# The last bias of a mixer layer: added by a TensorE pass, or into x by accumulating DMAs

## The chip, the cores and the metric

The kernel runs on one core of a Trainium2 chip. The metric is device time in microseconds (us) of one execution. Engines are named as in the profile: PE is TensorE's matmul side and PEld its weight loads, DVE is VectorE, ACT ScalarE, POOL GpSimd, and SP SyncE, which here only issues DMAs. An engine works through its instructions in the order in which they were written for it and waits on semaphores for what others produce. DMAs issued by SP and by POOL are carried out by the same 16 DMA engines. Only POOL issues the DMAs that add to their destination instead of overwriting it.

## The reference, cut to what matters

The input is 8 images of 128 x 128 pixels and 64 channels, in float32. The first layer is an attention along rows and columns. The second, the mixer, has two halves for each image, and the change lies in the very last term:

```python
h  = _pw(_ln(x, g1, b1), w_te, b_te)                  # 64 -> 128 channels
F  = fft2(h);  fc = gelu(_pw([re F, im F], w_fc, b_fc))
x1 = x + _pw(real(ifft2(fc)), w_tp, b_tp)
h2 = _pw(_ln(x1, g2, b2), w_fe, b_fe)                 # 64 -> 128 channels
d  = gelu(conv3x3_depthwise(h2, w_dw) + b_dw)
return x1 + _pw(d, w_fp, b_fp)                        # 128 -> 64, and the bias b_fp
```

`_pw` is a matrix product over the channels plus a bias. `b_fp` has 64 values; each is added to one channel of every pixel.

## The kernel before, in words

**Attention** (to about 1277 us) goes over tasks of 32 rows or columns. In its first four tasks it also runs the four steps of `preparation`, which fold weights and biases into a packed table in DRAM. The step `first` (from line 176) splits `b_fp` into three bf16 parts, so that their sum keeps the precision, repeats them for 8 rows and stores them in DRAM as `thirds` (line 192).

**The mixer** (from line 679) works image by image, in two parts that overlap: while `transforms(b)` runs for image b, mostly on PE, `mlp(b-1)` runs for the image before, mostly on DVE. One image's x, 128 x 128 x 64 in float32, stays in SBUF (32 KB on each of 128 partitions; a partition is a column of the image), in two buffers that take turns.

`transforms`: `along_w` and `along_h` (PE) are the Fourier transforms, `channels` (PE, L859), `bend` (ACT, L869) and `hermite` (POOL, L875) the middle layer with its gelu, `project`, `inverse_h` and `inverse_w` (PE) the way back, and `add` (DVE, L935) adds the result to x. This makes x1.

`mlp` takes x1 in 16 chunks of 8 lines, and a small 17th for the last line:

- `norm` sums each pixel's channels on DVE (L949, L950) and takes the inverse roots.
- `scale` (POOL, L1060) multiplies 8 lines of x by the roots, `turn` (PE) transposes them, `keep_x` (ACT) copies them, `expand` (PE) and `keep_e` (ACT) make h2.
- The depthwise convolution has nine taps. ACT does the first; one or two more are made by ACT as products, which DMAs add up (`gather`, POOL, L1153: an accumulating DMA of 512 KB from SBUF to SBUF); the other six or seven are `tap` on DVE (L1159).
- `bend` (ACT, L1206) is the gelu, and `shrink` (PE, L1215 ff.) the last product. It begins with a bf16 matmul over three rows (L1219), which writes the bias to all of the chunk's output in PSUM; 32 float32 matmuls (L1225) then accumulate onto it.
- `add` (DVE, L1230) reads PSUM and x, writes `ot`, and `store` (SP) sends it out. The output of chunk k is lines 8k-1 to 8k+6, one line behind its input.

In the last image half of the chunks do their convolution on PE instead.

The order on each engine is written by a planner. Every step is a task with an estimated cost, the tasks it follows, a due time, and the buffer slots that it takes and frees (`SLOTS`: four PSUM slots "mm" are shared by seven kinds of step, `shrink` among them). The planner repeatedly looks for the earliest start on each engine and, of those that could start within 0.3 us of it, takes the one due first. Due times come from the constants in line 47: image b's work begins at b times `PERIOD`, group i of the transforms is due `GROUP0 + GROUP * i` later, inverse group i `BACK0 + BACK * i`, chunk k of the mlp `CHUNK0 + CHUNK * k`. `lag` is the time that a DMA is taken to need until it lands. The planner's costs decide only the order; on the chip the engines wait for semaphores.

Of the kernel before, what the change touches and what calls it, by code (L numbers as in the profile page):

```python
# [22 lines left out]
F32 = mybir.dt.float32  # L23
BF16 = mybir.dt.bfloat16
I32 = mybir.dt.int32
AF = mybir.ActivationFunctionType
ALU = mybir.AluOpType
# [4 lines left out]
P = 128  # L32
C = 64
# [10 lines left out]
BY_DMA, BY_DMA_LAST = (1, 2), 1  # L44


PERIOD, GROUP0, GROUP, BACK0, BACK, CHUNK0, CHUNK, STAY, LOADX = 262.0, 0.5, 10.2, 174.8, 4.7, 22.4, 13.9, 0.0, -10.2
CH = 8
LN = 16

# [79 lines left out]
    return out  # L130


def preparation(nc, pool, ps, ident, prm, marks, packed, thirds):

    (g1, b1, g2, b2, w_te, b_te, w_fc, b_fc, w_tp, b_tp, w_fe, b_fe, w_dw, b_dw, w_fp, b_fp) = prm
    HW = float(P * P)
    v, dma = nc.vector, nc.sync.dma_start
# [5 lines left out]
    def cut(rows, cols):  # L143
        at[0] += cols
        return tmp[0:rows, at[0] - cols : at[0]]
# [18 lines left out]
    dma(out=f["wdw"], in_=w_dw.rearrange("a b o d -> d (a b o)"))  # L164
    dma(out=f["bdw"], in_=b_dw.unsqueeze(1))
    dma(out=f["wfp"], in_=w_fp)
    bfp = cut(3, C)
    dma(out=bfp, in_=b_fp.unsqueeze(0).to_broadcast([3, C]))

    split = pool.tile([3, CH * C + P + 3 * C], BF16, tag="split", name="split", bufs=1)  # L170
    dma(out=wrow, in_=w_dw.rearrange("a b o d -> (o a b) d").unsqueeze(0).to_broadcast([P, 9, HID]))
    dma(out=f["mark"], in_=marks[0:2, 0:8])
    dma(out=f["line"], in_=marks[:, 8 : 8 + P])
    hold = {}

    def first():
        parts = split[:, CH * C + P :].rearrange("p (n c) -> p n c", n=3)
        row = cut(3, C)
        for n in range(3):
            v.tensor_copy(parts[:, n, :], bfp)  # L180
            if n < 2:
                v.tensor_tensor(bfp, bfp, parts[:, n, :], ALU.subtract)
        v.tensor_scalar_mul(row, parts[:, 0, :], ident[0:3, 0:1])
        for n in range(1, 3):
            v.scalar_tensor_tensor(
                out=row, in0=parts[:, n, :], scalar=ident[0:3, n : n + 1], in1=row, op0=ALU.mult, op1=ALU.add
            )
        v.tensor_copy(
            split[:, 0 : CH * C].rearrange("p (n c) -> p n c", n=CH), row.unsqueeze(1).to_broadcast([3, CH, C])
        )  # L190
        nc.gpsimd.memset(split[:, CH * C : CH * C + P], 1.0)
        nc.gpsimd.dma_start(out=thirds, in_=split[:, 0 : CH * C + P])

        v.tensor_copy(f["ident"], ident)
        v.tensor_scalar(cen, ident[0:C, 0:C], -1.0 / C, None, ALU.add)
        v.tensor_scalar_mul(f["wtpn"], f["wtp"], -0.5)
        v.tensor_scalar_mul(f["wtp"], f["wtp"], 0.5)

        p = hold["a"] = ps.tile([P, 8, P], F32, tag="ps", name="pa")
        nc.tensor.matmul(p[:, 0, 0:1], lhsT=wte, rhs=col[:, 1:2], start=True, stop=True)  # L200
        nc.tensor.matmul(p[:, 0, 1:2], lhsT=wfr, rhs=col[:, 3:4], start=True, stop=True)
        v.tensor_scalar(u, p[:, 0, 0:1], bte, HW, ALU.add, ALU.mult)
        v.tensor_scalar(f["bfe"], p[:, 0, 1:2], bfe0, None, ALU.add)
        v.tensor_scalar_mul(wfr, wfr, col[:, 2:3])
        v.tensor_scalar_mul(wte, wte, col[:, 0:1])
# [52 lines left out]
    return [first, second, third, fourth]  # L258


def attention(tc, nc, x, w_q, b_q, w_k, b_k, w_v, b_v, gamma, x2, xn, prm, marks, packed, thirds):
    NB = x.shape[0]
    with ExitStack() as ctx:
        const = ctx.enter_context(tc.tile_pool(name="a_const", bufs=1))
# [4 lines left out]
        late = ctx.enter_context(tc.tile_pool(name="a_late", bufs=2))  # L269
        xw = ctx.enter_context(tc.tile_pool(name="a_xw", bufs=6))  # L270

        ps = ctx.enter_context(tc.tile_pool(name="a_ps", bufs=4, space=PSUM))
# [18 lines left out]
        ident = const.tile([P, P], F32, tag="ident", name="ident")  # L291
# [47 lines left out]
        for n in range(3):  # L339
            v = const.tile([P, R, C + 1], F32, tag="v%d" % n, name="v")  # L340
# [270 lines left out]


        fetch(1)
        prepare = preparation(nc, late, ps, ident, prm, marks, packed, thirds)
        N = len(tasks)
        E = mybir.EngineType
        with tc.manual_schedule(engines={E.PE, E.Activation, E.DVE, E.Pool}):
# [58 lines left out]
                flush(1)  # L676


def mixer(tc, nc, x2, xn, tbl, packed, thirds, out):
    NB = out.shape[0]  # L680
    with ExitStack() as ctx:
        const = ctx.enter_context(tc.tile_pool(name="m_const", bufs=1))
# [8 lines left out]
        rw, cos, sin, nsin, cosn, sinn, nsinn, idw = (tb[:, P * i : P * i + P] for i in range(8))  # L691
        pk = const.tile([P, PACKED], F32, tag="pk", name="pk")
        nc.sync.dma_start(out=pk, in_=packed[:, 0:PACKED])
        bias = const.tile([3, CH * C + P], BF16, tag="bias", name="bias")
        nc.sync.dma_start(out=bias, in_=thirds)
        c = fields(pk, PARTS)
        ident, wplus, wminus, dc, bfc, wtp, wtpn, btp, e0, wfe = (
            c[n] for n in ("ident", "wplus", "wminus", "dc", "bfc", "wtp", "wtpn", "btp", "e0", "wfe")
# [98 lines left out]
        plan = Plan()  # L797
# [249 lines left out]
        class Mlp:  # L1047
# [30 lines left out]
            def blank(self):  # L1078
# [2 lines left out]
                    nc.gpsimd.memset(t[:, :, P + 1 : P + 2], 0.0)  # L1081
                nc.gpsimd.memset(self.ring[0][:, 0, 1 : P + 1], 0.0)

            def turn(self, k):
                xc = self.xc.pop(k)
                tp = self.ps["t", k] = ps_m.tile([P, 4, P], F32, tag="mm", name="tpn")
                for j in range(4):
                    nc.tensor.transpose(
                        tp[:, j, :], xc[:, 2 * j : 2 * j + 2, :].rearrange("p s c -> p (s c)"), ident
                    )  # L1090
# [124 lines left out]
            def shrink(self, k):  # L1215
                i0, i1, r0 = self.rows(k)
                acc = self.acc.pop(k)
                op = self.ps["o", k] = ps_m.tile([P, CH, C], F32, tag="mm", name="op")
                nc.tensor.matmul(  # L1219
                    op[:, i0:i1, :].rearrange("p i c -> p (i c)"), lhsT=bias[:, CH * C : CH * C + P],  # L1220
                    rhs=bias[:, i0 * C : i1 * C], start=True, stop=False,
                )
                for i in range(i0, i1):
                    for z in (slice(0, 64), slice(64, 128)):
                        nc.tensor.matmul(op[z, i, :], lhsT=acc[:, i, z], rhs=wfp, start=False, stop=i == i1 - 1)  # L1225

            def add(self, k):
                i0, i1, r0 = self.rows(k)
# [11 lines left out]
        def mlp(b):  # L1240
# [5 lines left out]
            start = plan.add("SP", 0.0, lambda: m.__init__(b), im.added, t0 - 5)  # L1246
            root = norm(lambda: m.x, lambda: m.st, lambda h: t0 - 4 + h / 4, lambda h: [start])
            m.done = []
            e, ext, keep_x, users = None, None, [], []
            ready = start if b else plan.add("POOL", 0.8, lambda: m.borders(), [start], t0 - 30)  # L1250
            if last:

# [2 lines left out]
            for k in range(P // CH + 1):  # L1255
# [4 lines left out]
                if k < P // CH:  # L1260
                    xc, xt, s = Slot("xc"), Slot("xt"), Slot("mm")
                    takes = (s,) if last else (s, xt)
                    a = plan.add("POOL", 1.5, lambda k=k: m.scale(k), [root[k // 8]], t - 14, takes=(xc,))
                    p = plan.add("PE", 0.5, lambda k=k: m.turn(k), [a], t - 10, "F", takes, (xc,))
                    wait = []
                    if last:
                        wait = [keep_x[-1]] if k else [ext]
                        for n in (2, 3):
                            wait = wait + (users[-n] if len(users) >= n else [])
                    x_ = plan.add("ACT", 0.95 if last else 0.6, lambda k=k: m.keep_x(k), [p] + wait, t - 9, frees=(s,))  # L1270
                    keep_x.append(x_)
# [11 lines left out]
                else:  # L1283
# [24 lines left out]
                    for n in range(1, 1 + by_dma):  # L1308
                        s = Slot("pr")
                        a = plan.add("ACT", 1.22, lambda k=k, n=n: m.product(k, n), [e, first], t - 1 + n, takes=(s,))  # L1310
                        read = [a]
                        if made is None:
                            made, slot = a, s
                        else:
                            made = plan.add(
                                "POOL", 1.0, lambda k=k, n=n: m.gather(k, n, 1), [a, made], t + 6 * n - 5, frees=(s,), lag=7.1
                            )
                    for n in range(1 + by_dma, 9):
                        g = plan.add(
# [3 lines left out]
                    last_e[(17 * b + k) % 3] = [g] + read  # L1323
                    if made is not None:
                        g = plan.add(
                            "POOL", 1.0, lambda k=k: m.gather(k, 1), [g, made], t + late + 4, frees=(slot,), lag=7.1
                        )
                    g = plan.add("ACT", 0.4 if small else 1.06, lambda k=k: m.bend(k), [g], t + late + 13 - 1.6 * by_dma)
                    t += late
                s, ot = Slot("mm"), Slot("ot")  # L1330
                p = plan.add("PE", 1.25, lambda k=k: m.shrink(k), [g], t + 15, "C", (s,), (acc,))
                d = plan.add("DVE", 0.7, lambda k=k: m.add(k), [p], t + 16, takes=(ot,), frees=(s,))
                m.done.append(d)
                plan.add("SP", 1.0, lambda k=k: m.store(k), [d], t + 16, frees=(ot,), lag=5.0)

# [8 lines left out]
@with_exitstack  # L1344
def attention_mixer_kernel(ctx: ExitStack, tc: tile.TileContext, x, w_q, b_q, w_k, b_k, w_v, b_v, gamma, *rest):
    nc = tc.nc
    *prm, tbl, marks, out = rest
    NB = x.shape[0]
    dram = ctx.enter_context(tc.tile_pool(name="dram", bufs=1, space=DRAM))
    x2 = [dram.tile([P, P, C], F32, tag="x2_%d" % b, name="x2_%d" % b) for b in range(NB)]  # L1350
    xn = [dram.tile([P, 2, C, 64], F32, tag="xn_%d" % b, name="xn_%d" % b) for b in range(NB)]
    packed = dram.tile([P, PACKED + ADDED], F32, tag="packed", name="packed")
    thirds = dram.tile([3, CH * C + P], BF16, tag="thirds", name="thirds")
    attention(tc, nc, x, w_q, b_q, w_k, b_k, w_v, b_v, gamma, x2, xn, prm, marks, packed, thirds)
    mixer(tc, nc, x2, xn, tbl, packed, thirds, out)


_INS = [
# [29 lines left out]
```

## Time and profile before

| | |
|---|---|
| three runs | 3218.33 us median, 3213.28 to 3226.0 |
| the profiled execution | 3221.41 us, of which 3219.6 is the span from the first to the last instruction |
| mean granted TensorE clock | 0.971 |
| busy: PE, DVE, ACT, POOL | 2944.8, 2548.9, 2100.1, 1561.0 us |
| attention, up to the first Fourier pass | 0 to 1277 us |
| one image of the mixer, in between | 229 to 237 us |
| from the last transform add to the end | about 140 us |

How to read what follows: a busy time is the time in which an engine worked; the rest it waited. A group's line gives the instruction's source line, engine, operation, output and inputs, shapes and count, then busy time, the mean of one in ns, the idle time just before, and who ended it. A waits line reads "engine tile line <- releaser: us in total, times, longest". The chain of waits is followed back from the last instruction of the program, at each step to what released it; it tells which work the end hung on. In a windows line the columns are the window, its length, the busy us (and number) of PE, PEld, DVE, ACT and POOL, the granted clock, the share of the DMA engines and GB/s.

### The profile page before, as it was taken

Reading aid. Unit: us, or ns where it says so; the run is one execution under the profiler, and the core shown is the slowest. Engines: PE = TensorE matmul, PEld = TensorE weight load, DVE = VectorE, ACT = ScalarE, POOL = GpSimd, SP = SyncE. Lnnn points to the kernel's source line nnn. Section 1 sums busy time; section 2 is a strip of 40 time slices with the busy share of each in tenths; the row PEclk is TensorE's granted clock in tenths of the full one; section 3 lists DMA queues with packets and bytes.
Section 4 is the critical chain, followed back from the end, with each engine's and each line's share of the span. In section 5 each row is a group of like instructions: output and inputs, shape, how many; then the busy total and the mean of one; then the engine's idle time right before and its main releaser. Section 6 shows DMA issues by size and latency. Waiting matters only on the chain.

```text
span 3219.6 us, 110523 instructions
## 1 busy us (share of the span) xinstructions
PE 2944.8 (91%) x50612; PEld 2142.9 (67%) x50612; DVE 2548.9 (79%) x2322; ACT 2100.1 (65%) x2744; POOL 1561.0 (48%) x1944
## 2 busy tenths in 40 slices
PE   7998888988888987999999899999899999999978
PEld 6877777777777776666576576575566575665644
DVE  4574747474756567719999999999999999999996
ACT  3665656565655655538868768768668678677654
POOL 1095959595958585414515415515415425335321
PEclk8999999999999998999999999999999999999989
DMA  6024242434333323232552653643634634634433
GB/s 174 23 95 129 99 120 95 128 97 136 108 107 120 95 94 135 101 123 40 144 134 50 157 110 66 158 93 73 161 83 89 156 84 93 151 77 81 96 62 75
DMA packets 222458, 339.17 MB, mean 105 GB/s; under 512 B 142879, under 2 KB 176296, under 8 KB 207528
## 3 DMA queue, kind: packets, MB, share of 16 engines
q0 software_dynamic: 32496, 154.84, 20.4%
q1 hardware_dynamic: 188728, 177.19, 19.4%
q8 instruction: 397, 6.50, 0.8%
q14 instruction: 69, 0.57, 0.1%
q10 hardware_dynamic: 768, 0.07, 0.0%
HBM read 137.40 MB, written 102.25 MB: 74 GB/s over the span
## 4 chain that ended last, share of the span: by engine, by line
PE 52%; DVE 33%; issue 6%; POOL 6%; ACT 1%; DMA 1%; SPq 0%; POOLq 0%; DVEq 0%; ACTq 0%
DVE acc L1159 23%; PE yp L422 6%; PE fcps L859 5%; PE e L452 4%; PE dps L927 3%; PE yps L914 3%; PE vps L400 3%; DVE m L457 3%; PE tp L367 3%; PE pq L381 3%; PE yps L916 3%; PE tpy L603 2%; POOL xb L563 2%; PE op L1225 2%; PE aps L819 2%
## 5 line engine op out<-in xcount | busy, mean ns | idle before, releaser
L1159 DVE SCALAR_TENSOR_TENSOR acc<-h,pk,acc 128x1024 f32<-128x1024 f32 x840 | 1332.6, 1591 | 34.8 <-ACT acc L1145 13.3
L875 POOL TENSOR_TENSOR gs<-gl 128x512 f32<-128x512 f32 (+2 forms) x272 | 418.7, 1593 | 245.3 <-ACT gl L869 234.4
L859 PE MATMUL fcps<-f,pk 128*128 128x512 f32 (+2 forms) x1088 | 499.4, 591 | 0.0
L457 DVE TENSOR_REDUCE m<-e 128x8 f32<-128x1024 f32 x256 | 300.9, 1211 | 207.0 <-PE e L452 206.4
L1153 POOL DMA_DIRECT2D acc<-pr x120 | 105.6, 880 | 644.8 <-DVE acc L1159 428.1
L869 ACT ACTIVATE gl<-fcps,pk 128x1024 f32<-128x1024 f32 (+2 forms) x272 | 291.1, 1074 | 118.1 <-PE fcps L859 95.6
L463 ACT ACTIVATE att<-e 128x1024 f32<-128x1024 f32 x256 | 259.7, 1024 | 165.3 <-PE e L452 161.5
L422 PEld LDWEIGHTS yp<-v,att 128*64 128x64 f32 x8192 | 270.3, 143 | 89.1 <-issue 42.2
L1060 POOL TENSOR_TENSOR xc<-x,st 128x512 f32<-128x512 f32 x128 | 183.7, 1440 | 286.5 <-DVE st L101 186.1
L859 PEld LDWEIGHTS fcps<-f,pk 128*128 128x128 f32 x1088 | 190.5, 190 | 197.3 <-issue 162.8
L452 PE MATMUL e<-kt,qt 32*128 32x128 f32 x4096 | 298.4, 288 | 23.8 <-DVE v L403 12.7
L422 PE MATMUL yp<-v,att 128*64 128x65 f32 x8192 | 298.3, 230 | 20.6 <-issue 18.7
L452 PE MATMUL e<-qt,kt 32*128 32x128 f32 x4096 | 297.0, 286 | 15.6 <-issue 13.5
L452 PEld LDWEIGHTS e<-kt,qt 32*128 32x128 f32 x4096 | 257.9, 191 | 44.4 <-issue 21.2
L452 PEld LDWEIGHTS e<-qt,kt 32*128 32x128 f32 x4096 | 255.3, 191 | 20.2 <-issue 13.9
L1149 ACT ACTIVATE pr<-h,pk 128x1024 f32<-128x1024 f32 x176 | 214.1, 1236 | 0.0
L899 PEld LDWEIGHTS gps<-pk,gs 128*64 128x64 f32 x4032 | 135.5, 141 | 116.5 <-issue 65.5
L403 DVE TENSOR_TENSOR v<-vps,bv 128x1024 f32<-128x1024 f32 x128 | 155.9, 1218 | 66.9 <-PE vps L400 66.8
L914 PE MATMUL yps<-tb,gt 128*64 128x128 f32 x1024 | 200.8, 278 | 3.0 <-DVE ot L1230 2.4
L400 PE MATMUL vps<-wv,xt 64*64 64x64 f32 x8192 | 158.9, 228 | 46.6 <-DVE m L457 27.7
L915 PE MATMUL yps<-tb,gt 128*64 128x128 f32 x1024 | 200.8, 278 | 0.0
L842 PE MATMUL fps<-tb,at 128*64 128x128 f32 x1008 | 196.3, 277 | 0.0
(226 smaller groups left out, 7424.5 us busy)
## 6 DMA issues: line engine op xcount, KB each, us to landing
acc<-pr POOLq DMA_DIRECT2D x120, 512.0 KB, 5.4
xb<-in_x_dram SPq DMA_DIRECT2D x32, 1024.0 KB
xn<-xn SPq DMA_DIRECT2D x32, 1024.0 KB
x<-x SPq DMA_DIRECT2D x32, 1024.0 KB
x<-xb POOLq DMA_DIRECT2D x30, 1024.0 KB, 6.0
out_dram<-ot SPq DMA_DIRECT2D x120, 256.0 KB
xn<-yw POOLq DMA_DIRECT2D x14, 2048.0 KB, 9.4
pr<-pr POOLq DMA_DIRECT2D x56, 512.0 KB, 6.4
```

The lines of the kernel that those rows point to most:

```text
L400: nc.tensor.matmul(vps[z, s, j, :], lhsT=self.xts[t][rows, j, z], rhs=wv[rows, :], start=True, stop=True)
L422: nc.tensor.matmul(yq[z, q, j, :], lhsT=att[:, q, j, z], rhs=self.v[:, r, :], start=True, stop=True)
L452: nc.tensor.matmul(e[:, q, j, :], lhsT=left[rows, 4 * a + j, :], rhs=right[rows, 4 * a + j, :], start=not msk, stop=j == 3 or not msk,)
L457: nc.vector.tensor_reduce(new.mneg[:, 2 * k : 2 * k + 2, 4 * a : 4 * a + 4], e1, AX.X, ALU.max, negate=True,)
L463: nc.scalar.activation(att, e2, AF.Exp)
L859: nc.tensor.matmul(ps[:, sgn, 0:n], lhsT=w[:, cols], rhs=fv, start=True, stop=not mean)
L869: nc.scalar.activation(gl[:, :, 0:n], ps[:, :, 0:n], AF.Gelu, bias=bfc[:, half : half + 1])
L875: nc.gpsimd.tensor_tensor(gs[:, 0:n], gl[:, 0, 0:n], gl[:, 1, 0:n], ALU.add if half == 0 else ALU.subtract)
L914: nc.tensor.matmul(yps[0:64, c, :], lhsT=gr, rhs=cosn, start=True, stop=False)
L915: nc.tensor.matmul(yps[64:128, c, :], lhsT=gi, rhs=cosn, start=True, stop=False)
L1149: nc.scalar.activation(pr, self.lines(k, t), AF.Identity, bias=zero, scale=wdw[:, t : t + 1])
L1159: nc.vector.scalar_tensor_tensor(out=a, in0=self.lines(k, t), scalar=wdw[:, t : t + 1], in1=a, op0=ALU.mult, op1=ALU.add)
```

## The change

The bias pass in `shrink` goes, and with it `thirds`, its preparation and its tile; the 32 matmuls of a chunk now each start their own sum. Instead `b_fp` is written at the very start to a DRAM table `spread` of 32 x 64 values (32 copies). In `mlp`, a new step `offset(n)` on POOL adds this table, 8 KB to each of the 128 partitions, to 32 lines of x by one accumulating DMA of 1 MB. It is planned after the `scale` of chunks 3, 7, 11 and 15, since `scale` must read x without the bias, and with a lag of 9.0. `add(k)` waits for the offsets of the lines that it reads: a chunk reads into a new block of 32 lines at k = 4, 8 and 12, and the first chunk waits for the first block. The adds are therefore handed to the planner after all chunks. `PERIOD` stays; the other due constants, `shrink`'s cost (1.25 to 1.0) and the gathers' lag (7.1 to 7.0) change.

```diff
-PERIOD, GROUP0, GROUP, BACK0, BACK, CHUNK0, CHUNK, STAY, LOADX = 262.0, 0.5, 10.2, 174.8, 4.7, 22.4, 13.9, 0.0, -10.2
+PERIOD, GROUP0, GROUP, BACK0, BACK = 262.0, -1.9, 10.3, 174.8, 4.3
+CHUNK0, CHUNK, STAY, LOADX = 18.2, 14.2, 0.1, -10.2
...
     def first():
-        parts = split[:, CH * C + P :].rearrange("p (n c) -> p n c", n=3)
...
-        nc.gpsimd.dma_start(out=thirds, in_=split[:, 0 : CH * C + P])
...
+            def offset(self, n):
+
+                lines = self.x[:, 32 * n : 32 * n + 32, :].rearrange("p h c -> p (h c)")
+                b = spread.rearrange("a c -> (a c)").unsqueeze(0).to_broadcast([P, 32 * C])
+                nc.gpsimd.dma_start(out=lines, in_=b, accum_op=ALU.add)
...
             def shrink(self, k):
-                nc.tensor.matmul(
-                    op[:, i0:i1, :].rearrange("p i c -> p (i c)"), lhsT=bias[:, CH * C : CH * C + P],
-                    rhs=bias[:, i0 * C : i1 * C], start=True, stop=False,
-                )
                 for i in range(i0, i1):
                     for z in (slice(0, 64), slice(64, 128)):
-                        nc.tensor.matmul(op[z, i, :], lhsT=acc[:, i, z], rhs=wfp, start=False, stop=i == i1 - 1)
+                        nc.tensor.matmul(op[z, i, :], lhsT=acc[:, i, z], rhs=wfp, start=True, stop=True)
...
                     a = plan.add("POOL", 1.5, lambda k=k: m.scale(k), [root[k // 8]], t - 14, takes=(xc,))
+                    if k % 4 == 3:
+                        off.append(plan.add("POOL", 1.0, lambda k=k: m.offset(k // 4), [a], t - 13, lag=9.0))
...
-                p = plan.add("PE", 1.25, lambda k=k: m.shrink(k), [g], t + 15, "C", (s,), (acc,))
-                d = plan.add("DVE", 0.7, lambda k=k: m.add(k), [p], t + 16, takes=(ot,), frees=(s,))
+                p = plan.add("PE", 1.0, lambda k=k: m.shrink(k), [g], t + 15, "C", (s,), (acc,))
+                adds.append((k, p, s, ot, t))
+            for k, p, s, ot, t in adds:
+                ends = {max(8 * k - 1, 0) // 32, min(8 * k + 6, P - 1) // 32}
+                d = plan.add("DVE", 0.7, lambda k=k: m.add(k), [p] + [off[n] for n in sorted(ends)], t + 16, takes=(ot,), frees=(s,))
...
+    spread = dram.tile([32, C], F32, tag="spread", name="spread")
+    nc.sync.dma_start(out=spread, in_=prm[-1].unsqueeze(0).to_broadcast([32, C]))
```

## The prediction

> **What bounds the kernel now.** I read the page's busy times first, then the forty slices. The attention half (to 1277 us) has a full TensorE; in the mixer half TensorE and VectorE are full together.
>
> ```profile
> PE 2944.8 (91%) x50612; PEld 2142.9 (67%) x50612; DVE 2548.9 (79%) x2322; ACT 2100.1 (65%) x2744; POOL 1561.0 (48%) x1944
> ...
> PE   7998888988888987999999899999899999999978
> DVE  4574747474756567719999999999999999999996
> ```
>
> Everything that the change touches lies in the mixer, so I cut it by image with the windows view (window: length, then busy us of PE, PEld, DVE, ACT, POOL).
>
> ```profile
> 1682.70:1915.60 232.90, 221.18 (x2643) 146.91 (x2640) 223.78 (x189) 173.71 (x231) 89.60 (x76) 0.99 0.48 110
> 1915.60:2148.60 233.00, 221.47 (x2643) 147.69 (x2639) 221.51 (x189) 173.97 (x231) 93.75 (x76) 0.99 0.49 110
> 2384.30:2614.00 229.70, 218.68 (x2641) 145.30 (x2639) 220.97 (x189) 173.42 (x231) 91.32 (x76) 1.00 0.49 111
> 3080.00:3219.60 139.60, 117.06 (x905) 62.77 (x901) 104.86 (x115) 66.23 (x99) 28.28 (x24) 0.90 0.33 63
> ```
>
> An image takes about 233 us; DVE is busy for 221 to 224 of them, PE for 219 to 221. Neither can be called the bound alone, so I asked what each waits for, from 1682 to 2843 (DVE) and from 1450 to 3080 (PE).
>
> ```profile
> DVE ot L1230 <- PE op L1225: 19.6, 19, 1.5
> DVE x L935 <- PE dps L927: 7.1, 15, 0.9
> DVE acc L1159 <- ACT acc L1145: 4.2, 8, 0.6
> ```
>
> ```profile
> PE gps L899 <- DVE ot L1230: 28.2, 12, 5.5
> PE op L1225 <- ACT acc L1206: 18.2, 13, 3.9
> PE gps L899 <- POOL gs L875: 15.1, 25, 1.6
> ```
>
> DVE waits 31 us over five images, 6 per image; the rest of its idle time is some 36 ns between dependent taps. PE's longest wait is for DVE: a PSUM slot that comes free only when the output add has read it. So DVE sets the pace for most of an image, and PE where the inverse transform runs (the chain changes over near the middle).
>
> DVE's busy time is not all its own. The taps (L1159, 128x1024) have a median of 1.28 us and a mean of 1.68. Of the 784, the 51 that run beside a DMA issue of POOL alone take 1.28 us as well, the 210 beside POOL's tensor_tensors 1.90.
>
> ```profile
> 2001.15 0.68 DVE L1230 TENSOR_TENSOR ot<-op,x 128x512 f32<-128x512 f32 x1
> 2001.75 14.69 DVE L1159 SCALAR_TENSOR_TENSOR acc<-h,pk,acc 128x1024 f32<-128x1024 f32 x6
> ```
>
> Six taps took 14.7 us here instead of 7.7, while POOL, released by a gather, ran two hermites and two scales back to back. That stretch is some 40 us of each image's DVE time, and the change removes no POOL arithmetic.
>
> **The change, step by step.** The sum is made against the profiled execution, 3221.4 us (span 3219.6), which lies 3.1 us above the median of the three runs, 3218.3.
>
> *The bias pass goes.* There are 136 passes, of 385 ns as drawn; the chain shows what one costs PE's stream, the distance to the next start:
>
> ```profile
> 2090.97 0.32 PE op L1219
> 2091.29 1.08 PE op L1225 x32
> 2092.37 1.91 PE dps L927 x4
> ```
>
> Some 0.315 x 136 = 43 us of PE time (fewer columns in 16 of them, so rather less). All of it would be gained if PE alone set the time. Where DVE sets it, PE only waits longer for its slot. The pieces of the chain of waits that are named PE op L1219 add up to 19.3 us: 1.6 to 3.2 in each of the seven image windows from 1450 to 3080 (15.2 together) and 4.1 in the last stage, where PE does half of the convolutions. I take 19.3, because DVE's row (95% busy, 6 us of real waits per image) is nearer to a bound than PE's; ends: 0 and 43.
>
> *Four accumulating DMAs per image come.* Issue: a gather's issue is the nearest row.
>
> ```profile
> L1153 POOL DMA_DIRECT2D acc<-pr x120: 860/882/936, 1488.2 to 3206.8; - x120
> ...
> DMA to landing us min/median/max: 4.5/5.6/12.0
> ```
>
> 32 x 0.88 = 28 us of POOL, 3.5 per image, against 140 idle us of POOL in each; beside an issue taps do not stretch (row above), so DVE does not pay. What stands behind one on POOL is a hermite or a gather, late by 0.9 us. I take 0; if each came at a moment when PE waits for gs, 28 us.
>
> Landing: the trace's accumulating packets of 4 KB take a median of 0.34 us, 128 of them on 16 engines 2.8 us; so a landing of 5.6 is 2.8 of transfer and 2.8 of the rest. 1 MB in packets of 8 KB, doubled: 5.6 + 2.8 = 8.4 us, an estimate. No row accumulates from DRAM, or from one row sent to all partitions. The nearest is the load of w_dw, one DRAM row of 4608 B to 128 partitions: all packets inside 2.9 us, median 0.18 us each, no slower than other loads of that size. Bounds: 6.0 us (the median of the plain 1 MB store x<-xb) and 12.8, the gather's worst landing plus the second 0.5 MB at the median's cost (12.0 less 5.6, plus 6.4).
>
> The Trainium skill has a cheaper rule (DMA: Bandwidth & Descriptors, "Anatomy of one DMA"): 2.0 us plus bytes over 436 GB/s, an estimate of 4.4 us here. This case's 512 KB gather takes 5.6 where it gives 3.2. By the rule, or by the rows, the step below costs the same nothing.
>
> *The add gets a wait.* Only the adds of chunks 0, 4, 8 and 12 wait for a new landing; behind a waiting add on DVE stand all the taps and dps adds that follow, and for those wait POOL's gathers, ACT's bends and PE. In the image from 1915.6 the fourth, eighth, twelfth and sixteenth scales end at 1941.0, 1992.7, 2045.8 and 2095.9; the adds start at 1962.1, 2016.4, 2070.5 and 2114.7. The margins are 21, 24, 25 and 19 us. The offset needs 0.9 + 8.4, after at most two hermites that the new order puts ahead of it (4.5 us at 2045.8): 14 of 19 or more. Cost 0; at the upper landing 18 of 19, still 0. In the last image the margins are 24, 32, 15 and 14 us, counted by the order of adds; at the upper landing (0.9 + 12.8) nothing is left over, and I allow 4.
>
> *Other transfers.* 32 x 5.6 us on all engines is 22 us per image against a DMA share of 0.48. A gather issued right behind an offset waits for the rest of it. In the new order a gather follows directly on the third and fourth offset of an image, but it waits for a tap first: in the trace the next gathers go out 10 us (2055.9) and 7 us (2103.3) after those scales. Expected delay 1 to 3 us, on a gather that ACT waits for in 37 of 127 cases. I take 0 to 2 us per image, centre 0; upper end: two gathers per image, each the whole 5.6 us late and on the chain, 8 x 11 = 90 us.
>
> A rule that speaks against the change stands in the Trainium skill (SBUF — State Buffer, "SBUF: two separate sides"): a DMA issued by GpSimd that takes some 620 ns alone takes some 3100 while VectorE works in a mode that holds the shared port. By that each offset would land an estimated 2.5 us later, still inside the margins, and the sum would not move. The trace does not show the trap beside taps: gathers issue in 860 to 936 ns and land in a median of 5.6 us.
>
> *Preparation.* Nine tiny DVE instructions (L180 to L188, 173 to 416 ns, 2.2 us), a memset and a DMA go in attention, where DVE has idle time: 0, at best 2.2. The new write of the spread table stands ahead of the first load on SP: one issue, 0.4 us (row: 0.40 for that load). +0.4.
>
> *Due times.* The order changes on every engine. On DVE the add of chunk 0 moves from behind 13 taps to behind 16, that of chunk 1 from 20 or 21 to 23, of chunk 4 from 40 to 39; the last transform add stands ahead of the small taps instead of among them. On PE the shrink of chunk 0 comes after twelve channel passes instead of ten, so slot and add move together. What an order is worth, no row tells; windows of nearly one order run from 229.0 to 235.7 us, some 3 either side. I take 0 and keep 3 us per image, 7 x 3 = 21 us, either way.
>
> Sum: 3221.4 - 19.3 + 0.4 = 3202.5; less the 3.1 by which that execution lies high: **3199 us**.
>
> **The rivals.**
> - *The relief counts in full.* PE's time goes down by 43 us and the new order uses it. For it: the chain lies on PE for 97 to 141 us in the middle images, and DVE waits 20 us for op. Against: DVE has only 6 us of waits per image, 7 x 6 = 42 at the very best, with 4 more in the last stage. 3218 - 43 = 3175, or down to 3160 with a better order.
> - *Nothing comes of it.* PE idles instead, and the new bunching of POOL's tensor_tensors stretches the taps by 2 to 3 us per image more. 3218, 3208 to 3234. One 7.4 us tap per image, as at 2001.8, is enough.
> - *Slower: offsets hold up gathers.* Place: the software DMA queue, behind the third and fourth offset; price 5.6 us each at most, then bend, shrink and add late, PE's slot held, DVE stopped at the add. It decides from about 2.5 us on the chain per image (20 us in eight). Half of the price on one gather more than the slack gives 8 x 5.6 = 45: 3199 + 45 = 3244. For it: ACT already waits 72 us for landings. Against: 7 to 10 us between issue times.
>
> **How the numbers follow.** Direct gain alone 0.42 (3199, own range 3185 to 3210), full relief 0.19 (3160 to 3185), nothing 0.15 (3208 to 3234), slower 0.24 (3234 to 3290). Half a per cent, 16 us, is about what a measurement of this kernel can tell from no change: the limits are 3202 and 3234. Below 3202 lie 0.19 and six tenths of 0.42: 0.44; between, 0.17 + 0.15: 0.32; above, 0.24. The range leaves out about a tenth at each end (half of the full relief, four tenths of slower): 3170 to 3255.
>
> **What would show it.** Right: PE busy in an image down by 5 to 6 us, DVE busy unchanged within 3, no rows of an add waiting for x's DMA; offsets landing in 7 to 10 us; periods of 229 to 231. Wrong: landings over 15 us; "DVE ot" waiting for the DMA; acc L1206 waiting for gathers well over 72 us in all; the taps' mean away from 1.68 by over 0.03 (30 ns x 784 = 24 us, more than the whole forecast).

## The result and the profile after

The changed kernel takes **3200.8 us** (median of nine runs, 3187.9 to 3209.1) against 3213.3 for the kernel before (nine runs beside it, 3202.4 to 3226.0): a ratio of **0.996, interval 0.9942 to 0.9979**. Two later comparisons gave 0.9948 (0.9932 to 0.9963) and 0.9949 (0.9928 to 0.9969). By the medians it is 12 to 20 us faster, with a forecast of 19 (as a ratio, 0.994), and the forecast of 3199 us is 2 us off the first median. How far the steps behind it hold is another matter.

The page of the changed kernel, busy times and slices:

```profile
PE 2915.1 (91%) x50476; PEld 2144.6 (67%) x50476; DVE 2486.9 (78%) x2313; ACT 2096.0 (66%) x2744; POOL 1636.0 (51%) x1974
...
PE   7998898988888986999999999999999999999978
...
DVE  4575747574747576819999999999999999999996
```

PE is busy for 30 us less, as intended; but DVE is too, by 62, although the change takes next to nothing from it. The windows by image (window: length, then busy us of PE, PEld, DVE, ACT, POOL):

```profile
1667.10:1896.00 228.90, 216.26 (x2624) 146.02 (x2622) 213.82 (x190) 173.39 (x230) 100.92 (x80) 0.98 0.60 130
1896.00:2126.70 230.70, 217.48 (x2624) 147.48 (x2622) 214.11 (x190) 173.02 (x230) 101.29 (x80) 0.97 0.59 129
2126.70:2355.30 228.60, 217.03 (x2624) 147.05 (x2622) 213.33 (x190) 172.98 (x230) 101.99 (x80) 0.97 0.60 130
3047.70:3196.40 148.70, 115.32 (x906) 63.41 (x906) 114.35 (x128) 70.25 (x104) 31.46 (x30) 0.89 0.49 93
```

An image takes 229 to 231 us, some 3 less than before; PE is busy for 216 to 217 of them (before 219 to 221), DVE for 213 to 214 (before 221 to 224). The last stage, from the last transform add to the end, is 148.7 us long. In the profile before, that stage was 144.8 us (from 3074.9; the window shown there starts later). So the images gain and the last stage gives some back.

The waits of DVE and of PE from 1450 to 3080 (releaser, us in total, times, longest), DVE's first of before, then of after, and PE's of after:

```profile
DVE ot L1230 <- PE op L1225: 23.3, 25, 1.5
DVE x L935 <- PE dps L927: 11.1, 22, 0.9
DVE acc L1159 <- ACT acc L1145: 6.1, 10, 1.3
```

```profile
DVE ot L1211 <- PE op L1206: 48.8, 44, 4.9
DVE x L914 <- PE dps L906: 16.8, 29, 0.9
DVE acc L1144 <- ACT acc L1130: 14.5, 14, 1.3
```

```profile
PE gps L878 <- DVE ot L1211: 24.1, 10, 3.4
PE fps L820 <- DVE ot L1211: 23.3, 6, 3.9
PE op L1206 <- ACT acc L1191: 19.6, 14, 5.3
```

No add waits for the offsets' DMA; most of the new waits on DVE are for PE. Where DVE's busy time went is in the group of the large taps (busy, mean ns of one, idle before), first of before, then of after:

```profile
L1159 DVE SCALAR_TENSOR_TENSOR acc<-h,pk,acc 128x1024 f32<-128x1024 f32 x784 | 1313.1, 1679 | 33.1 <-ACT acc L1145 13.3
```

```profile
L1144 DVE SCALAR_TENSOR_TENSOR acc<-h,pk,acc 128x1024 f32<-128x1024 f32 x784 | 1250.4, 1601 | 47.4 <-ACT acc L1130 28.1
```

The same 784 taps are 63 us shorter. The 210 (before) and 232 (after) that overlap only POOL's tensor_tensors have means of 1.90 and 1.86 us, those beside an issue alone 1.28 in both; but the taps of over 3 us, single ones stretched to as much as 7.4 us by several POOL instructions in a row, went from 52 (251 us together) to 22 (90 us). The next table holds, of each profile, the six images from the first Fourier pass of the second image to that of the eighth; there DVE's busy time, its waits and the short gaps between its instructions make up the length:

| kernel | six images | DVE busy | of it large taps | DVE waits | PE busy |
|---|---|---|---|---|---|
| before | 1391.5 | 1334.2 | 1058.9 | 35.6 | 1322.8 |
| after | 1372.6 | 1280.3 | 1005.7 | 70.5 | 1297.8 |
| after, two more profiles | 1375.3, 1379.8 | 1272.6, 1279.5 | 996.8, 1004.1 | 80.8, 78.7 | 1296.9, 1299.9 |

(The waits column leaves out idle times too short for the waits view, some 22 us in each kernel.) DVE is busy for 54 to 62 us less and waits 35 to 45 more; 12 to 19 us remain. The scatter between profiles of one kernel, 7 us here, bounds what such a table can tell.

The offsets themselves, by the view of their source line:

```profile
L1067 POOL DMA_DIRECT2D x<-spread x32: 883/890/1209, 1477.1 to 3154.8; - x32
...
DMA to landing us min/median/max: 7.9/8.4/9.6
```

The median landing of 8.4 us is the value estimated from the accumulating 4 KB packets. The cheaper rule in the Trainium skill (DMA: Bandwidth & Descriptors, "Anatomy of one DMA"), 2.0 us plus bytes over 436 GB/s, gave an estimate of 4.4 us; the measurement decides for the rows. The skill's warning in SBUF — State Buffer ("SBUF: two separate sides"), that a DMA issued from GpSimd can be held up for microseconds while VectorE works in a mode that holds the shared port, is not seen here: the issues took 883 to 1209 ns beside busy taps. Whether the taps work in such a mode no run shows.

### The profile page after: what moved, and what is told of

The parts are those of the page before. It is cut to its first block, busy times and chain, and to the rows that moved or that the text cites. A ratio compares the mean times of both kernels' runs of the same rounds, so it can differ in the third digit from the quotient of the medians.

```text
span 3196.4 us, 110388 instructions
## 1 busy us (share of the span) xinstructions
PE 2915.1 (91%) x50476; PEld 2144.6 (67%) x50476; DVE 2486.9 (78%) x2313; ACT 2096.0 (66%) x2744; POOL 1636.0 (51%) x1974
## 4 chain that ended last, share of the span: by engine, by line
PE 49%; DVE 29%; POOL 9%; issue 6%; DMA 4%; ACT 2%; SPq 0%; POOLq 0%; ACTq 0%; DVEq 0%
DVE acc L1144 16%; PE fcps L838 6%; PE yp L403 6%; PE e L433 4%; PE dps L906 4%; POOL xb L544 3%; PE yps L893 3%; PE yps L895 3%; DVE m L438 3%; PE vps L381 3%; PE tp L348 3%; DMA acc<-pr 3%; PE pq L362 3%; PE op L1206 3%; PE tpy L584 2%
## 5 line engine op out<-in xcount | busy, mean ns | idle before, releaser
L1144 DVE SCALAR_TENSOR_TENSOR acc<-h,pk,acc 128x1024 f32<-128x1024 f32 x840 | 1270.0, 1517 | 49.6 <-ACT acc L1130 28.1
L854 POOL TENSOR_TENSOR gs<-gl 128x512 f32<-128x512 f32 (+2 forms) x272 | 441.9, 1644 | 303.3 <-ACT gl L848 301.9
L838 PE MATMUL fcps<-f,pk 128*128 128x512 f32 (+2 forms) x1088 | 508.9, 598 | 0.2 <-ACT f L828 0.2
L433 PE MATMUL e<-qt,kt 32*128 32x128 f32 x4096 | 300.1, 288 | 12.2 <-issue 10.1
L1115 ACT ACTIVATE h<-hp,pk 128x512 f32<-128x512 f32 x254 | 156.4, 669 | 71.4 <-PE hp L1095 71.2
```

What stands on the lines that cost most here:

```text
L433: nc.tensor.matmul(e[:, q, j, :], lhsT=left[rows, 4 * a + j, :], rhs=right[rows, 4 * a + j, :], start=not msk, stop=j == 3 or not msk,)
L838: nc.tensor.matmul(ps[:, sgn, 0:n], lhsT=w[:, cols], rhs=fv, start=True, stop=not mean)
L854: nc.gpsimd.tensor_tensor(gs[:, 0:n], gl[:, 0, 0:n], gl[:, 1, 0:n], ALU.add if half == 0 else ALU.subtract)
L1144: nc.vector.scalar_tensor_tensor(out=a, in0=self.lines(k, t), scalar=wdw[:, t : t + 1], in1=a, op0=ALU.mult, op1=ALU.add)
```

## The experiments

Each ratio below is against the kernel before, run beside the experiment on the same chip in five rounds.

### The pass alone, without the move

The theory: the pass is worth its share of the chain, 19 us. Edit of the kernel before (its planned order is untouched):

```diff
             def shrink(self, k):
...
-                nc.tensor.matmul(
-                    op[:, i0:i1, :].rearrange("p i c -> p (i c)"), lhsT=bias[:, CH * C : CH * C + P],
-                    rhs=bias[:, i0 * C : i1 * C], start=True, stop=False,
-                )
...
-                        nc.tensor.matmul(op[z, i, :], lhsT=acc[:, i, z], rhs=wfp, start=False, stop=i == i1 - 1)
+                        nc.tensor.matmul(op[z, i, :], lhsT=acc[:, i, z], rhs=wfp, start=True, stop=True)
```

> The kernel before with the bias pass left out of every shrink (the output then lacks the last bias), no offsets, and the order of before on every engine. Theory, as in the prediction: what the pass is worth is its part of the chain of waits, 19 us, in whatever order; 0.994 of before, about 3194 against 3213. Rival 1 (the new order did it): DVE sets the time and PE only waits longer, so 0 to 5 us, 0.999 or more, with the taps' mean still near 1.68 us. Rival 2 (full relief): 43 us, 0.987.

Measured: 3202.1 against 3218.6 us, **0.995 (0.993 to 0.997)**: 16 us, 10 to 23 by the interval. PE's busy time in the six images falls by 27 us (1322.8 to 1295.6), the length by 14.5; the last stage falls from 144.8 to 142.0. The chain's 19.3 was a good price, and the 43 us of PE time a bad one. By which route the 16 us arrive one profile can't say: DVE's waits stay at 34 us, and its taps are 12 us shorter, which is little more than the 9 us between profiles of one kernel.

The same pass put back into the changed kernel, with a bias of zeros so that it costs its time and adds nothing, and with the new order and the offsets kept:

```diff
+        bias = const.tile([3, CH * C + P], BF16, tag="bias", name="bias")
+        nc.vector.memset(bias, 0.0)
...
+                nc.tensor.matmul(
+                    op[:, i0:i1, :].rearrange("p i c -> p (i c)"), lhsT=bias[:, CH * C : CH * C + P],
+                    rhs=bias[:, i0 * C : i1 * C], start=True, stop=False,
+                )
...
-                        nc.tensor.matmul(op[z, i, :], lhsT=acc[:, i, z], rhs=wfp, start=True, stop=True)
+                        nc.tensor.matmul(op[z, i, :], lhsT=acc[:, i, z], rhs=wfp, start=False, stop=i == i1 - 1)
```

> The changed kernel with a bf16 pass of zeros put back at the head of every shrink; offsets and order as in the changed kernel. Theory: the pass costs its 19 us here too, so this takes 1.002 of before, 0.006 more than the changed kernel. Rival 1: the order keeps the gain, 0.996 as the changed kernel. Rival 2: 43 us come back, 1.009.

Measured: 3211.2 us, 0.9982 (0.9965 to 0.9998). Against the 0.9948 to 0.996 of the changed kernel that is 7 to 11 us, each ratio being known to some 5 or 6 us; so whether the pass costs less in the new order than the 16 us in the old one is not settled. In the one profile the six images are 2 to 10 us longer than the changed kernel's, with PE busy for some 26 us more, and the last stage takes 154.4 us instead of 146.6 to 148.7: much of the pass's cost in the new order falls there. DVE's large taps are at 1005.8 us in the six images here too, so their shortening does not come from the pass.

### The offsets left out, shortened, and moved

The changed kernel with an empty `offset`; the order of everything else stays:

```diff
             def offset(self, n):
...
-                nc.gpsimd.dma_start(out=lines, in_=b, accum_op=ALU.add)
+                pass
```

> The changed kernel with the offsets left out (the output then lacks the last bias); the order stays. Theory: the offsets cost nothing, so 0.996 of before, as the changed kernel. Rival 3 (the offsets hold up gathers): without them the gathers land as before (three quarters within 6.0 us instead of 7.6), ACT waits less for them, and the time falls by another 10 us or more, 0.993.

Measured: 3195.9 against 3218.6 us, **0.9926 (0.9907 to 0.9945)**: the 32 offsets cost 7 to 11 us of the changed kernel's time, with some 6 us of uncertainty in each ratio. The six images take 1377.6 us without them, and 1372.6, 1375.3 and 1379.8 with them: nothing to be seen there. The last stage takes 142.7 us instead of 146.6 to 148.7:

```profile
3050.50:3193.21 142.71, 113.77 (x906) 62.90 (x906) 114.16 (x127) 70.52 (x104) 27.59 (x26) 0.90 0.34 67
```

That is 4 to 6 us in one place. The remaining few are not located, and may be scatter; the length of attention alone differs by 9 us between the three profiles of the changed kernel.

The changed kernel's chain of waits in the last stage (start, us, what) names the place; these are all of its DMA entries there:

```profile
3047.05 5.32 DMA acc<-pr
...
3087.75 8.06 DMA acc<-pr
...
3155.44 10.19 DMA acc<-pr
...
3183.20 5.78 DMA acc<-pr
```

Two gathers on the chain take 8.1 and 10.2 us; the other two take 5.3 and 5.8. On POOL (start, us, instruction, idle before and releaser), each stands right behind an offset:

```profile
3085.10 0.90 POOL L1067 DMA_DIRECT2D x<-spread  x1 [0.30 <-POOL xc L1039]
3087.75 0.89 POOL L1138 DMA_DIRECT2D acc<-pr  x1 [1.75 <-issue]
...
3154.85 0.88 POOL L1067 DMA_DIRECT2D x<-spread  x1 [0.31 <-POOL xc L1039]
3155.44 1.19 POOL L1138 DMA_DIRECT2D acc<-pr  x1
```

Without the offsets the same gathers land after 4.6 and 4.5 us, and the chain of that kernel holds only the first and the last DMA:

```profile
3049.84 5.30 DMA acc<-pr
...
3180.04 5.69 DMA acc<-pr
```

If it is the transfer that holds the gathers up, and not the issue or the wait, an offset of one line (32 KB instead of 1 MB) should be free:

```diff
-                lines = self.x[:, 32 * n : 32 * n + 32, :].rearrange("p h c -> p (h c)")
-                b = spread.rearrange("a c -> (a c)").unsqueeze(0).to_broadcast([P, 32 * C])
+                lines = self.x[:, 32 * n : 32 * n + 1, :].rearrange("p h c -> p (h c)")
+                b = spread[0:1, :].rearrange("a c -> (a c)").unsqueeze(0).to_broadcast([P, C])
```

> The changed kernel with each offset cut to its first line, 32 KB instead of 1 MB (the other lines lack the last bias): POOL still issues 32 DMAs and the adds still wait, but next to nothing is transferred. If the transfers cost the time: as without offsets, 0.993 of before, the last stage 143 us. If POOL's issues or the waits cost it: as the changed kernel, 0.996, 148 us.

Measured: 3196.6 us, 0.9945 (0.9931 to 0.9958). The last stage takes 142.8 us, as without offsets, with every issue and every wait still there, so it is the transfer that costs the stage its 4 to 6 us:

```profile
3060.72:3203.52 142.80, 113.24 (x906) 62.73 (x906) 114.36 (x128) 70.64 (x104) 30.10 (x30) 0.90 0.35 68
```

The whole time, however, lies no lower than the changed kernel's 0.9948; a gain of 4 us is at the edge of what the ratio resolves, and only the stage shows it.

A first attempt at a remedy was to cut the last image's offsets into sixteen of 8 lines, one behind each scale, so that none is long:

```diff
...
-                    if k % 4 == 3:
+                    if last:
+                        off.append(plan.add("POOL", 1.0, lambda k=k: m.offset(k, 8), [a], t - 13, lag=5.0))
+                    elif k % 4 == 3:
...
-                ends = {max(8 * k - 1, 0) // 32, min(8 * k + 6, P - 1) // 32}
+                size = 8 if last else 32
+                ends = {max(8 * k - 1, 0) // size, min(8 * k + 6, P - 1) // size}
```

> The changed kernel, with the offsets of the last image cut into 16 of 8 lines, one behind each scale. Theory: the offsets cost nothing in the earlier images and 6 us in the last, where gathers go out right behind them and wait for 1 MB; behind a quarter of a MB they land in under 7 us, and the time from the last transform add to the end falls from 148.7 to 143 to 145 us: 4 to 6 us less than the changed kernel in all. Rival (they cost in every image): the last stage gains, but the total stays 10 us above the kernel without offsets. Rival (POOL's issues count): twelve issues more delay the scales, and the last stage gets no shorter.

Measured: 3208.9 against 3214.5 us, 0.9984 (0.997 to 0.9998); the last stage is 155.2 us long, longer than with four large ones, although no gather of it takes over 6.6 us to land. POOL shows a part of why, right behind the last transform adds:

```profile
3066.63 0.89 POOL L1067 DMA_DIRECT2D x<-spread  x1 [0.30 <-POOL xc L1039]
3067.24 1.35 POOL L1039 TENSOR_TENSOR xc<-x,st 128x512 f32<-128x512 f32 x1
3068.90 0.90 POOL L1067 DMA_DIRECT2D x<-spread  x1 [0.30 <-POOL xc L1039]
3069.51 1.35 POOL L1039 TENSOR_TENSOR xc<-x,st 128x512 f32<-128x512 f32 x1
```

An offset must wait until the scale just before it has finished (0.30 us), and its issue puts off the next scale: a scale comes every 2.3 us instead of every 1.0 to 1.3, so all that the scales feed starts later: the sixth scale begins 37.1 us after the last transform add, in the changed kernel 32.6 to 32.9. These 4 us go with the issues. The stage as a whole is 6 to 9 us longer than the changed kernel's, but in this kernel the planner also put other instructions of DVE, ACT and POOL in another order, and the clock granted in the stage was 0.85 instead of 0.88 to 0.90; how the rest divides is not shown.

The other remedy leaves the offsets whole and sends the short gather first. In the last image, the offsets behind the scales of chunks 7 and 15 are planned after the gathers of chunks 0 and 10; nothing else moves:

```diff
+            held, sent = [], {}
...
-                    if k % 4 == 3:
+                    if k % 4 == 3 and last:
+                        held.append((k, a, t))
+                    elif k % 4 == 3:
...
+                        sent[k] = g
...
+            for k, a, t in held:
+                first = [sent[n] for n in {7: [0], 15: [10]}.get(k, [])]
+                off.append(plan.add("POOL", 1.0, lambda k=k: m.offset(k // 4), [a] + first, t - 13, lag=9.0))
```

> The changed kernel, with the second and the fourth offset of the last image issued after the gather that stood right behind each; nothing else moves. Theory: these gathers land in about 5.5 us instead of 8 to 10, and the time from the last transform add to the end falls from 147 or 148 us to 143: 4 us less than the changed kernel, 0.994 of before. Rival: the adds then wait for the offsets, or the last image hangs on PE anyway: no less than the changed kernel.

Measured: 3194.3 against 3216.7 us, **0.9934 (0.9909 to 0.9958)**. POOL's order in the last stage:

```profile
3074.88 0.89 POOL L1138 DMA_DIRECT2D acc<-pr  x1 [2.94 <-issue]
3075.46 1.22 POOL L1067 DMA_DIRECT2D x<-spread  x1
...
3139.68 0.87 POOL L1138 DMA_DIRECT2D acc<-pr  x1
3140.28 1.18 POOL L1067 DMA_DIRECT2D x<-spread  x1
```

The two gathers land after 4.8 us each; the offsets land after 9.8 and 9.9 instead, and no add waits for them. The stage takes 142.9 us; the changed kernel, run beside it, takes 147.4:

```profile
3034.86:3177.73 142.87, 113.60 (x906) 62.73 (x906) 114.05 (x128) 70.52 (x104) 31.41 (x30) 0.90 0.51 97
```

This is the best of the kernels here that compute the whole result. The ratios of the two, 0.9934 and 0.9949, have overlapping intervals; only the stage shows the gain of some 4 us. The clock granted in the stage was 0.90 here and 0.88 in the changed kernel beside it; at 0.90 another profile of the changed kernel took 146.6 us, so the clock is not the cause.

### The order

The new constants without the new tasks: the kernel before, with its bias pass, and only the due constants and the lag of the gathers (both places, one is shown):

```diff
-PERIOD, GROUP0, GROUP, BACK0, BACK, CHUNK0, CHUNK, STAY, LOADX = 262.0, 0.5, 10.2, 174.8, 4.7, 22.4, 13.9, 0.0, -10.2
+PERIOD, GROUP0, GROUP, BACK0, BACK = 262.0, -1.9, 10.3, 174.8, 4.3
+CHUNK0, CHUNK, STAY, LOADX = 18.2, 14.2, 0.1, -10.2
...
-                            "POOL", 1.0, lambda k=k: m.gather(k, 1), [g, made], t + late + 4, frees=(slot,), lag=7.1
+                            "POOL", 1.0, lambda k=k: m.gather(k, 1), [g, made], t + late + 4, frees=(slot,), lag=7.0
```

> The kernel before with the bias pass kept and only the new due constants and the gathers' lag of 7.0. Theory: an order is worth nothing by itself, within 5 us of before. Rival 1 (the new order did it): the taps beside POOL's arithmetic stretch less, their mean falls from 1.68 to about 1.60 us as in the changed kernel, and the time by 10 us or more, 0.996.

Measured: 3250.0 against 3218.6 us, **1.0095 (1.0079 to 1.0112)**: 31 us slower, though the taps are shorter than before (1617 ns on average, 1014.9 us in the six images). DVE's waits from 1450 to 3080:

```profile
DVE ot L1231 <- PE op L1226: 42.8, 41, 2.9
DVE acc L1160 <- ACT acc L1146: 39.7, 21, 2.9
DVE x L936 <- PE dps L928: 34.0, 52, 1.7
```

In the six images DVE is busy for 42 us less than in the kernel before and waits 70 us more; the images take 28 us longer. Short taps are no gain by themselves.

The other half of the cross: the changed kernel with the old constants (the gathers' lag of 7.0 stays).

```diff
-PERIOD, GROUP0, GROUP, BACK0, BACK = 262.0, -1.9, 10.3, 174.8, 4.3
-CHUNK0, CHUNK, STAY, LOADX = 18.2, 14.2, 0.1, -10.2
+PERIOD, GROUP0, GROUP, BACK0, BACK = 262.0, 0.5, 10.2, 174.8, 4.7
+CHUNK0, CHUNK, STAY, LOADX = 22.4, 13.9, 0.0, -10.2
```

> The changed kernel with the due constants of before. Theory: the constants were worth little here; the pass and the offsets decide, so within 5 us of the changed kernel. Rival (the new constants suit only the kernel with offsets, as they cost 31 us without them): 10 us or more slower than the changed kernel, 1.000 of before or above.

Measured: 3283.0 against 3214.5 us, **1.0209 (1.0192 to 1.0227)**, 68 us slower than before. ACT's wait for the gathers from 1450 to 2820, here and in the changed kernel:

```profile
ACT acc L1191 <- DMA acc<-pr: 72.2, 32, 7.1
```

```profile
ACT acc L1191 <- DMA acc<-pr: 23.8, 18, 3.4
```

It is three times as long, and PE's shrinks wait 56.8 us for the bends behind it (from 1450 to 3080), against 19.6 in the changed kernel. That looked like the third rival, the offsets in the gathers' way; to see how much of the 68 us it is, the same kernel with an empty `offset`:

```diff
             def offset(self, n):
...
-                nc.gpsimd.dma_start(out=lines, in_=b, accum_op=ALU.add)
+                pass
```

> The kernel of the old due constants with offsets, in its own order, with the offsets left out (the output lacks the last bias). Theory: the offsets hold up gathers that this order leaves no room behind (ACT waits 72 us for gathers from 1450 to 2820 us, 24 in the changed kernel); without them most of the 68 us lost come back, 1.003 of before or less. Rival (the order alone is bad, PE stands at shrinks that come too early in it): 1.015 or more, the offsets worth no more than in the changed kernel, about 5 us.

Measured: 3255.7 against 3216.7 us, 1.013 (1.0109 to 1.0151): still some 40 us slower than before. So in that order the offsets cost 0.0079, some 25 us (known to some 9), and the order itself the larger part. ACT's wait for the gathers from 1450 to 2820, in this kernel and in the kernel before:

```profile
ACT acc L1189 <- DMA acc<-pr: 67.2, 26, 7.8
```

```profile
ACT acc L1206 <- DMA acc<-pr: 51.0, 27, 4.4
```

So of the 72 us in that stretch only 5 go with the offsets; the long wait belongs to the order. From the second image to the end of the program the wait is 111.6 us with the offsets and 90.5 without. These 21 us are near the 25 that the offsets cost there, but that they cost it by this route was not tested. Of the 33 us between the two profiles 14 lie in the six images and 10.5 in the last stage. Put together, in ratios to the kernel before:

| constants | old tasks, with the pass | new tasks, no offsets issued | new tasks, offsets |
|---|---|---|---|
| old | 1 | 1.013 | 1.0209 |
| new | 1.0095 | 0.9926 | 0.9948 to 0.996 |

The new constants are 65 us better for the new tasks (1.013 to 0.9926) and 31 us worse for the old (1 to 1.0095). Neither set is better in itself. Which constant does it, and through which of the planner's choices, was not tried.

### The taps beside POOL

The prediction's reading that POOL stretches DVE's taps was put to the test on the kernel before: the hermite, which reads the two halves of a tile, is replaced by a memset of its output.

```diff
-                nc.gpsimd.tensor_tensor(
-                    gs[:, 0:n], gl[:, 0, 0:n], gl[:, 1, 0:n], ALU.add if half == 0 else ALU.subtract
-                )
+                nc.gpsimd.memset(gs[:, 0:n], 0.0)
```

> The kernel before with every hermite replaced by a memset of the same tile (its output is not the mixer's any more): POOL keeps its instructions, but reads nothing of gl; order kept. Theory (the taps' stretch beside POOL's reading sets DVE's pace): the taps' mean falls from 1.68 to under 1.45 us, DVE's busy time per image by over 20 us, and the time by 60 us or more in all, until PE alone binds at 219 to 221 us per image: 0.975 to 0.981. Rival (PE sets the pace, DVE's stretch only fills its waiting time): less than 20 us, 0.994 or above, with DVE idle instead.

Measured: 3135.6 against 3216.7 us, **0.9752 (0.973 to 0.9773)**: 81 us. The groups of taps and of memsets:

```profile
L1157 DVE SCALAR_TENSOR_TENSOR acc<-h,pk,acc 128x1024 f32<-128x1024 f32 x784 | 1057.8, 1351 | 66.8 <-ACT acc L1143 46.0
...
L875 POOL MEMSET gs<- 128x512 f32 x240 | 143.3, 652 | 197.8 <-PE gps L897 155.8 <-PE gps L891 41.9
```

The taps' mean falls from 1679 to 1351 ns. The 60 taps beside a memset alone take 1.28 us on average, as those beside nothing. This agrees with the Trainium skill (SBUF — State Buffer, "SBUF: two separate sides"), by which an operation of VectorE with two SBUF inputs contends for the shared port pair only with a GpSimd operation that reads SBUF. One image of that kernel (window, length, PE, PEld, DVE, ACT, POOL):

```profile
1878.60:2098.50 219.90, 217.06 (x2638) 144.96 (x2637) 186.65 (x191) 173.49 (x230) 58.97 (x77) 1.00 0.51 116
```

PE is busy for 217 of 220 us: with DVE relieved, PE is the bound. The edit also takes 1 us from each of the 272 POOL instructions, so the 81 us are the effect of both, stretch and POOL's time.

### The changed kernel again

With nothing edited, beside the runs above:

> The changed kernel once more, beside the three below. From the last transform add to the end it should again take about 148 us, with a gather of 8 to 10 us behind the second and the fourth offset of the last image; 0.996 of before.

> The changed kernel beside the three above: 0.995 to 0.996 of before, 147 to 149 us from the last transform add to the end.

Measured: 3198.4 against 3214.5 us, 0.9948 (0.9932 to 0.9963), and 3196.9 against 3216.7, 0.9949 (0.9928 to 0.9969). Together with the first comparison these set the scatter of the ratio between comparisons, about 0.001. The last stage took 146.6 and 147.4 us. The gather behind the fourth offset landed after 10.1 and 9.8 us, as expected; the one behind the second, issued 4.0 us behind it and not 2.7, landed after 6.7 and 6.3, sooner than expected. In the first of these two profiles only this one of the two late gathers is on the chain.

## Why the prediction was right, and where it was not

- **"The bias pass goes", 19.3 us:** right in size: 16 us in the old order. The full relief (43 us) fell. In the new order the pass is worth 7 to 11, which the scatter does not tell from 16. PE's busy time per image fell by some 4 us, not 5 to 6.
- **Issue and landing of the offsets:** right. 0.89 us against 0.88, and 8.4 us against an estimate of 8.4. In the six images the offsets cost nothing that can be seen.
- **"The add gets a wait", cost 0, 4 allowed for the last image:** no add waits for an offset, neither in the images nor at the end. The last stage did lose 4 to 6 us, but that is not this step's doing.
- **"Other transfers", 0 to 2 us per image, centre 0:** this is the step that was mis-sized, in one place. Its premise, 7 to 10 us between an offset and the next gather, did not hold: in the full images the gathers behind the second and the third offset went out 3.2 and 4.1 us behind them and landed after 7.6 to 8.7 us, while the same gathers take 4.6 to 7.4 without offsets. Their bends waited for ten of these twelve gathers, 0.3 to 1.3 us each. That is near the price, and the images show no loss from it. The step did not ask whether the last image has the same room. There the gathers behind the second and the fourth offset landed late on the chain, after 8.1 and 10.2 us in the first profile; the offsets' transfers, which delay them, cost the stage its 4 to 6 us. The third rival's mechanism exists, then, at a tenth of its price. In the old constants' order the offsets cost some 25 us, by a route that was not tested.
- **"Due times", 0, 21 us either way:** this is the term that was wrong in kind. The order was priced as something that can be laid over either set of tasks. With the new tasks the new constants are worth 65 us, with the old ones they cost 31. The sum came out because a refit that goes with its tasks lost nothing: from the pass alone (0.995) to the new tasks and order without offsets (0.9926) it is 8 us of gain, though the two intervals overlap, and the offsets took 7 to 11 back. That two terms set at 0 nearly cancelled is luck.
- **"DVE busy unchanged within 3", "the taps' mean away from 1.68 by over 0.03" as a sign of being wrong:** both came out otherwise, some 9 us per image and 1.60 us. The shorter taps go mainly with the new constants: they are there with the pass put back, without the offsets, and with the constants alone; with the new tasks and the old constants the mean is 1.64 and, without offsets, 1.63 us, halfway. The step behind it, that the stretch is a fixed 40 us per image since POOL's arithmetic stays, failed: with the same arithmetic, taps of over 3 us went from 52 to 22, so it goes with how POOL's instructions fall beside taps. By that sign 24 us or more should have shown in the time; 53 to 62 us came off the large taps in the six images, and 35 to 45 came back as DVE's waits for PE and ACT. The 95% of DVE's row did not make it the bound by itself.
- **"Nothing comes of it":** fell: the intervals of all three comparisons lie below 1, and its bunching of POOL was seen with the opposite sign.

## What to carry to other kernels

Where two engines are both nearly full, price a removed instruction by its pieces on the chain of waits and not by its engine's busy time; here that gave 19 for a measured 16, instead of 43. Put a short DMA on which something waits ahead of a long one in the same queue (here the stage fell from 147.4 to 142.9 us), and look for the place where the pipeline ends, since the room that hid a late landing in the full images was not there. A refitted order belongs to its tasks: judge it by crossing old and new constants with old and new tasks, and expect that part of what shorter instructions save can come back as waits.

## What the runs showed of the hardware that I had not expected

- A 512 KB gather issued 0.6 us behind a 1 MB accumulating DMA lands after 9.8 to 10.2 us instead of 4.5; 2.7 us behind it, after 8.1 instead of 4.6; and 3.2 or 4.1 us behind it in the full images, after 7.6 to 8.7.
- Long taps are the expensive ones: 52 of 784 taps held 251 us in the kernel before, and the new order left 22 with 90 us. POOL writing without reading (the memset) does not stretch a tap: the 60 beside a memset alone took 1.28 us.
- Cutting a DMA into pieces has its price in issues: each offset of 8 lines took about 1.2 us of POOL's time, 0.3 of it a wait for the scale just before it, and after five of them POOL's scales were 4 us late.
